# A graph layer's messages: two silus in one ScalarE operation, edge addresses made once, and more columns copied per step

## The chip, the cores and the metric

The kernel runs on one core of a Trainium2 chip. The metric is the device time of one execution in microseconds (us), the median of the runs shown. The engines are TensorE (PE for its products, PEld for its weight loads), VectorE (DVE), ScalarE (ACT), GpSimd (POOL) and SyncE (SP, which only issues DMAs here). An engine's own queue, in which its register loads and its DMA issues stand, is written with a q: DVEq, ACTq, SPq.

## The reference

One layer of a message-passing network over 12500 nodes of 64 features and 400000 edges that are sorted by their target `dst`, with 16 features on each edge:

```
m_in = concatenate([x[src], x[dst], edge_attr], axis=-1)
h = silu(m_in @ W1 + b1)
messages = silu(h @ W2 + b2)
agg = segment_sum(messages, dst, num_segments=12500)
x = layernorm(x + silu(concatenate([x, agg]) @ W3 + b3))
```

W1 is 144 x 64. Its first 64 rows belong to x[src], the next 64 (called W1b here) to x[dst], the last 16 to the edge features.

## The kernel before

**Tiling.** The edges lie in 3125 tiles of 128. Eight tiles are an octet, and there are 391 octets; three octets are a chunk. One loop (line 644) runs over the octets, and inside it the order of the work on PE, ACT, DVE and SP is the order in which the code is written: each of these engines does its share of turn o in that order, and waits in that order. POOL runs by itself, up to three octets ahead. Because the edges are sorted, an octet's targets lie in a window of 48 consecutive nodes.

**First layer of an octet** (line 475). `xw` holds, for the window of the octet, x W1b of its 48 nodes (twice, for even and odd tiles) and W1's rows for the edge features; its product with `oh` (a 0/1 comparison of `dst` with the window's nodes, and the edge features under it) gives the target and edge parts of all 1024 edges in one PSUM bank, `p1` (line 482). The source part is added tile pair by tile pair. For most tiles POOL has fetched the rows of x W1a by indirect DMA from a table `pa` in DRAM, 128 rows an instruction (line 391), and PE adds them through the identity (line 495). The first 12 octets (RAW) fetch x itself, while the tables are still being made.

**Columns.** For about half of the octets the first tile pair isn't fetched by POOL. Its 256 columns of x transposed are copied out of `xs`, a copy of x in SBUF, into `cx`, one 64 x 4 byte copy per edge, by DVE (`tensor_reduce`, line 316) and by ACT (`copy`, line 318), and PE multiplies them by W1a (line 492). Each turn DVE copies 40 columns and then 32 (VCOLS), ACT 32 and 32 (ACOLS). The address of a column comes from a register: the registers are loaded up to eight at a time from a row of addresses (LOADS, line 299), and the eight copies follow. The row is fetched three turns ahead from `src_row` by SP (`index`, line 369) and is turned from node numbers to byte addresses by two small DVE operations (`address`, line 377). `xs` holds x twice, in partitions 0 to 63 and 64 to 127, and edges of the pair's second tile are copied from the upper half to the upper half of `cx`; so the two halves of an address row need different bases (XBASE). A few further tile pairs are fetched row by row by SP (line 342).

**Silus and second layer.** ACT applies silu with bias `b1s` to `p1` (line 499), giving `h`. One turn later PE forms b2 + h W2 in `p2` (lines 508 and 510), and ACT applies silu again (line 514), giving the messages `m`. One turn later again PE adds them up by node with the comparison `eh` (line 523, `add_up`), and two turns after that DVE adds the window's sums into `agg` (line 528, `add_window`).

**Order within turn o.** PE: the window product of o+1 (only for o+1 < 60), first layer of o, `add_up` of o-2, second layer of o-1. ACT: 32 columns, silu of o, 32 columns, silu of o-1. DVE: `add_window` of o-4, comparison `oh` of o+1 (line 465), 40 columns, comparison `eh` of o+1 (line 471), 32 columns, `address` of o+2 if an address row begins there. From octet 60 on, x W1b of a window is loaded by SP from a DRAM table `pw1b`, which is made in turns 8 to 57 (`table_b`); before that PE makes it from x (`window_product`) and DVE copies it (line 443).

**Node part.** As soon as a group of 512 nodes has all of its edges, PE forms its products with W3 (lines 555 to 558), ACT the silu (line 564), DVE the statistics and the division (lines 571 to 588), between the turns of the edges.

Of the kernel before, what the change touches and what calls it, by code (L numbers as in the profile page):

```python
# [20 lines left out]
P = 128  # L21
G = 4
CT = 24
OT = 8
# [7 lines left out]
TABLES = 7  # L32
ACOLS = (32, 32)
VCOLS = (40, 32)
ROWS = 16
LOADS = 8
XBASE = (0, 64 << 18)
XADDR = 36864
LAG = CT * P // 32
# [6 lines left out]
@with_exitstack  # L46
def kernel(
    ctx: ExitStack,
    tc: tile.TileContext,
    x: bass.AP,  # L50
    xt: bass.AP,
    src_c: bass.AP,
    src_row: bass.AP,
    dst_c: bass.AP,
    dst_row: bass.AP,
    attr_t: bass.AP,
    dst_2: bass.AP,
    attr_2: bass.AP,
    base: bass.AP,
    w1: bass.AP,  # L60
    b1: bass.AP,
    w2: bass.AP,
    b2: bass.AP,
    w3: bass.AP,
    b3: bass.AP,
    out: bass.AP,
    edges: int,
):

    nc = tc.nc
    N, D = x.shape

    const = ctx.enter_context(tc.tile_pool(name="const", bufs=1))
    dram = ctx.enter_context(tc.tile_pool(name="dram", bufs=1, space=DRAM))
    pa = dram.tile([N, D], F32, name="pa")

    pw1b = dram.tile([xt.shape[1], 2 * D], F32, name="pw1b")
    badi = const.tile([1, 1], I32, name="badi")
    ident = const.tile([P, P], F32, name="ident")  # L90
    make_identity(nc, ident)

    with ExitStack() as inner:
        windows(inner, tc, ident, badi, pa, pw1b, x, xt, src_c, src_row, dst_c, dst_row, attr_t, dst_2, attr_2, base, w1, b1, w2, b2, w3, b3, out, edges)

    flag = nc.values_load(badi[0:1, 0:1], min_val=0, max_val=2 * P,
                          skip_runtime_bounds_check_because="a count of partitions")
    with tc.If(flag > 0):
        general(tc, ident, x, xt, src_c, dst_c, dst_row, attr_t, w1, b1, w2, b2, w3, b3, out, edges)


def windows(ctx, tc, ident, badi, pa, pw1b, x, xt, src_c, src_row, dst_c, dst_row, attr_t, dst_2, attr_2, base, w1, b1, w2, b2, w3, b3, out, edges):
    nc = tc.nc
# [31 lines left out]
    nc.vector.memset(w1d, 0.0)  # L135
    b1s = const.tile([P, 1], F32, name="b1s")
    w2d = const.tile([P, P], F32, name="w2d")
    nc.vector.memset(w2d, 0.0)
    w3s = const.tile([P, D], F32, name="w3s")
    for s in range(2):  # L140
        h = slice(s * D, (s + 1) * D)
        nc.scalar.dma_start(w1d[h, h], w1[0:D, :])
        nc.scalar.dma_start(b1s[h, :], b1.rearrange("(k o) -> k o", o=1))
    XC = 2048
    xs = fast.tile([P, NP], F32, name="xs")

    def resident(s, c):
        w = min(XC, NP - c)
        nc.scalar.dma_start(xs[s * D:(s + 1) * D, c:c + w], xt[:, c:c + w])

    resident(0, 0)
    for s in range(2):
        h = slice(s * D, (s + 1) * D)
        nc.scalar.dma_start(w2d[h, h], w2)
    resident(0, XC)
    w3x = const.tile([D, D], F32, name="w3x")
# [38 lines left out]

    agg = fast.tile([P, NP], F32, name="agg")

    bf = fast.tile([1, NO], F32, name="bf")
# [58 lines left out]
    with tc.tile_pool(name="gat", bufs=AHEAD + 2) as gat, tc.tile_pool(name="drp", bufs=2) as drp, \  # L257
# [3 lines left out]
            tc.tile_pool(name="ps1", bufs=2, space=PSUM) as ps1, \  # L261
            tc.tile_pool(name="ps2", bufs=2, space=PSUM) as ps2, \
            tc.tile_pool(name="psa", bufs=1, space=PSUM) as psa, \
# [33 lines left out]
        def addresses(eng, j, e0, n):  # L297
            s = e0 // P
            _, regs = nc.values_load_multi_w_load_instructions(  # L299
                indices[j][0:1, e0:e0 + n], engines=(eng,), min_val=XBASE[s] + XADDR,  # L300
                max_val=XBASE[s] + XADDR + 4 * (N - 1), skip_runtime_bounds_check_because="src names a node")
            return regs

        def columns(o, eng, part):
            for j, e0, n in pieces(o, eng, part):
                regs = addresses(eng, j, e0, n)
                if pairs[j] not in cols:
                    cols[pairs[j]] = cx.tile([P, P], F32, name="cx")
                t = cols[pairs[j]].bitcast(U8)
                s = e0 // P  # L310
                h = slice(s * D, (s + 1) * D)
                for e, r in zip(range(e0 % P, e0 % P + n), regs):
                    to, frm = t[h, 4 * e:4 * e + 4], xb[h, ds(r - (XBASE[s] + XADDR), 4)]
                    if eng == ENG.DVE:

                        nc.vector.tensor_reduce(to, frm[:, :, None], AX.X, OP.max)  # L316
                    else:
                        nc.scalar.copy(to, frm)  # L318
# [46 lines left out]
        def index(o):  # L365
            for j in begun(o):
                t = cxi.tile([1, 2 * P], I32, name="cxi")
                e = octs[pairs[j]][1] * P
                nc.sync.dma_start(t, src_row[:, e:e + 2 * P])
                indices[j] = t  # L370

        def address(o):
            for j in begun(o):
                t = indices[j]
                for s in range(2):
                    h = slice(s * P, (s + 1) * P)
                    nc.vector.tensor_scalar(t[:, h], t[:, h], 4.0, float(XBASE[s] + XADDR), op0=OP.mult, op1=OP.add)  # L377

# [26 lines left out]
        def table_b(c):  # L405
# [5 lines left out]
            for i in range(k):  # L411
                p = min(P, n - i * P)
                nc.tensor.matmul(ps[:p, i, :], xs[0:D, c + i * P:c + i * P + p], w1ab[:, 1, :], start=True, stop=True)
            if n == 2 * P:
# [21 lines left out]
        def window_product(o):  # L436
            pw = mis.tile([P, P], F32, name="mm")
            nc.tensor.matmul(pw[:E, :], winrow[o].rearrange("k s w -> k (s w)"), w1bb.rearrange("k s m -> k (s m)"),
                             start=True, stop=True)
            winrow[o] = pw  # L440
# [14 lines left out]

        hots = {}

# [17 lines left out]
        def first_layer(o):  # L475
# [4 lines left out]
            oh, eh = hots.pop(o)  # L480
            p1 = ps1.tile([P, OT // 2, P], F32, name="p1")
            nc.tensor.matmul(p1[:, :k], xw[o % XWB], oh, start=True, stop=False, skip_group_check=True)  # L482
            if o < RAW:
                pt = mis.tile([P, OT // 2, P], F32, name="mm")
                for i in range(k):
                    nc.tensor.matmul(pt[:, i, :], ga[:, 2 * i:2 * i + 2, :].rearrange("p s d -> p (s d)"), ident,
                                     start=True, stop=True)
                xg = work.tile([P, OT // 2, P], F32, name="m")
                nc.vector.tensor_copy(xg[:, :k], pt[:, :k])
# [3 lines left out]
            for i in range(1 if o in pairs else 0, k if o >= RAW else 0):  # L493
                g2 = single.pop(o) if o in rpairs and i == 1 else ga[:, 2 * i:2 * i + 2, :]
                nc.tensor.matmul(p1[:, i, :], g2.rearrange("p s d -> p (s d)"), ident,  # L495
                                 start=False, stop=(i == k - 1), skip_group_check=True)
            columns(o, ENG.Activation, 0)
            h = work.tile([P, OT // 2, P], F32, name="h")
            nc.scalar.activation(h[:, :k], p1[:, :k], AF.Silu, bias=b1s)  # L499
            made[o] = h, eh  # L500

        def second_layer(o):
            c, t0, n, first, last = octs[o]
            n2 = n + n % 2
            k = n2 // 2
            h, eh = made.pop(o)
            p2 = ps2.tile([P, OT, D], F32, name="p2")
            nc.tensor.matmul(p2[:, :n2, :], one3, b2r[:, :n2, :], start=True, stop=False, skip_group_check=True)  # L508
            for i in range(k):
                nc.tensor.matmul(p2[:, 2 * i:2 * i + 2, :].rearrange("p s d -> p (s d)"), h[:, i, :], w2d,  # L510
                                 start=False, stop=(i == k - 1), skip_group_check=True)
            columns(o + 1, ENG.Activation, 1)
            m = work.tile([P, OT, D], F32, name="m")
            nc.scalar.activation(m[:, :n2], p2[:, :n2], AF.Silu)  # L514
            made[o] = m, eh

        def add_up(o):
            c, t0, n, first, last = octs[o]
            m, eh = made.pop(o)
            pg = sums[:, o % 4, :]  # L520
# [120 lines left out]
        with tc.manual_schedule(engines={ENG.PE, ENG.Activation, ENG.DVE, ENG.SP}):  # L641
            compare_dst(0)
            compare_nodes(0)
            for o in range(NO + 1):
                if o == 0:
                    sources(0, slice(CT, SCT))
                    nc.sync.dma_start(dc[:, CT:SCT], dst_c[:, CT:SCT])
                for k in parts[3 * o - 3:3 * o] if o else []:
                    n = min(XC, NP - k)
                    nc.scalar.activation(agg[:, k:k + n], zero.to_broadcast([P, n]), AF.Copy)  # L650
                if o < 2:
                    for c in parts[2:5] if o == 0 else parts[5:]:
                        resident(0, c)
                if o == 3:
# [6 lines left out]
                if o == RAW:  # L661
                    nc.vector.memset(mv, 1.0)
                    nc.vector.memset(eps, 1e-5)
                if 5 <= o < 5 + (len(parts) + 1) // 2:
                    for c in parts[(o - 5) * 2:(o - 4) * 2]:
                        resident(1, c)
                index(o + 3)
# [18 lines left out]
                if o < NO:  # L686
                    first_layer(o)
                if o == 0:
                    nc.vector.tensor_copy(b2r, b2p[:, None, :].to_broadcast([3, OT, D]))
# [14 lines left out]
                if o >= 1:  # L704
                    for c in tables[(o - 1) * per:o * per]:
                        table(c)
                if 8 <= o < 8 + len(tables_b):
                    table_b(tables_b[o - 8])
                if o >= 2:
                    add_up(o - 2)  # L710
                if o >= 1:
                    second_layer(o - 1)
                address(o + 2)
                raddress(o + 2)
# [296 lines left out]
```

## Time and profile before

| | |
|---|---|
| time, median of 3 runs | 3724.96 us (3719.63 to 3726.66) |
| time of the execution that was profiled | 3726.66 us |
| its span, first to last instruction | 3724.9 us |
| busy in the span: PE, PEld, DVE, ACT, POOL | 69%, 51%, 73%, 78%, 68% |
| granted TensorE clock | 0.712 |
| DMA: bytes moved, mean rate | 243.80 MB, 65 GB/s |

A row of the costliest groups reads: line, engine, operation, the tiles it writes and reads, how often; then its busy time and the mean duration of one; then the idle time of the engine just before such instructions and what ended most of it. Instructions of one kind overlap on DVE and ACT, so that the busy time of a group can be less than count times mean. "issue" means that the engine waited for nothing that the profile shows. The loop takes 9 to 10 us a turn after the first 150 us.

### The profile page before, as it was taken

To read this page: it belongs to the slowest core of one execution; us is meant where nothing else is said; L and a number is where in the kernel's file an instruction comes from. 1 tells how busy PE (TensorE), PEld (TensorE's weight loads), DVE (VectorE), ACT (ScalarE), POOL (GpSimd) and SP (SyncE) were. 2 spreads that over 40 slices of the span, in tenths; PEclk is the share of its full clock that TensorE was granted. 3 is DMA by queue.
4 is the path that set the end of the run, shared out by engine and by line. 5 is a ranking of instruction groups with operands and counts; after the bars stand their busy time and mean duration, and the time that the engine had idled before them with its cause. 6 is when DMAs were issued, how large, how long until landed. Compare 5 with 4: busy or idle time off the path is not lost. (4 is left out here: it accounts for less than half of the span.)

```text
span 3724.9 us, 112677 instructions
## 1 busy us (share of the span) xinstructions
PE 2581.7 (69%) x14667; PEld 1910.2 (51%) x14667; DVE 2703.3 (73%) x29014; ACT 2912.8 (78%) x24892; POOL 2535.2 (68%) x2690
## 2 busy tenths in 40 slices
PE   7878777767766667666666666667767666667666
PEld 5655555545544545454554555545545455445454
DVE  2477777777777777777777777777777777777775
ACT  2477878788787878878888878887888887887885
POOL 7777666676666766767666676676676666766763
PEclk8766667676667667777777777777766777776767
DMA  6533332322322232222232232232222222223222
GB/s 131 115 71 76 68 67 63 67 59 57 69 60 61 60 66 58 60 64 61 59 64 66 59 68 56 60 65 59 60 62 63 66 57 62 63 58 67 58 59 53
DMA packets 201259, 243.80 MB, mean 65 GB/s; under 512 B 87009, under 2 KB 139806, under 8 KB 199598
## 3 DMA queue, kind: packets, MB, share of 16 engines
q1 hardware_dynamic: 86336, 130.74, 15.0%
q0 software_dynamic: 85792, 88.02, 12.8%
q10 hardware_dynamic: 28366, 17.75, 1.9%
q14 instruction: 640, 5.24, 0.5%
q8 instruction: 125, 2.05, 0.2%
HBM read 223.41 MB, written 12.87 MB: 63 GB/s over the span
## 5 line engine op out<-in xcount | busy, mean ns | idle before, releaser
L391 POOL DMA_INDIRECT ga<-pa,sc x2585 | 2442.3, 945 | 1111.0 <-issue 683.9
L316 DVE TENSOR_REDUCE cx<-xs 64x4 uint8 x26944 | 2058.4, 148 | 813.8 <-issue 764.3
L318 ACT COPY cx<-xs 64x4 uint8 x24000 | 2403.6, 188 | 133.8 <-issue 102.2
L523 PE MATMUL pg<-eh,m 128*64 128x48 f32 x6250 | 357.2, 273 | 1047.3 <-DVE agg L528 996.7
L523 PEld LDWEIGHTS pg<-eh,m 128*64 128x64 f32 x6250 | 309.0, 184 | 1108.1 <-issue 630.5
L510 PE MATMUL p<-w2d,h 128*128 128x128 f32 x3126 | 743.6, 413 | 0.0
L510 PEld LDWEIGHTS p<-w2d,h 128*128 128x128 f32 x3126 | 633.9, 301 | 143.5 <-issue 143.5
L482 PE MATMUL p<-oh,xw 128*128 128x512 f32 (+1 forms) x782 | 672.8, 959 | 27.8 <-DVE xw L443 27.6
L514 ACT ACTIVATE m<-p 128x512 f32<-128x512 f32 x391 | 232.9, 596 | 443.1 <-PE p L510 427.4
L495 PEld LDWEIGHTS p<-ident,ga 128*128 128x128 f32 x2586 | 448.5, 248 | 160.5 <-issue 147.2
L495 PE MATMUL p<-ident,ga 128*128 128x128 f32 x2586 | 439.4, 321 | 0.0
L499 ACT ACTIVATE h<-p,b1s 128x512 f32<-128x512 f32 x391 | 267.1, 683 | 54.9 <-PE p L490 41.5
L465 DVE TENSOR_TENSOR oh<-dr,wrow 96x512 f32<-96x512 int32 x391 | 263.2, 673 | 2.8 <-DMA dr<-in_dst 2.8
L482 PEld LDWEIGHTS p<-oh,xw 128*128 128x128 f32 x782 | 197.9, 310 | 43.0 <-DVE xw L443 34.7
L471 DVE TENSOR_TENSOR eh<-wrow,dc 128x384 f32<-128x384 f32 x391 | 213.9, 547 | 2.4
L508 PE MATMUL p<-b2r,one 3*128 3x512 bf16 x391 | 207.1, 530 | 0.0
L492 PEld LDWEIGHTS p<-cx,w1d 128*128 128x128 f32 x398 | 115.6, 290 | 177.8 <-issue 177.8
L528 DVE TENSOR_TENSOR agg<-agg,pg 128x48 f32 x391 | 78.0, 200 | 102.6 <-PE pg L523 46.3
L391 POOL DMA_INDIRECT ga<-in_x,sc x96 | 90.8, 945 | 30.3 <-issue 27.4
L564 ACT ACTIVATE z<-mm 128x256 f32<-128x256 f32 (+1 forms) x25 | 9.6, 383 | 125.5 <-PE mm L558 125.5
L492 PE MATMUL p<-cx,w1d 128*128 128x128 f32 x398 | 104.6, 357 | 0.0
L377 DVE TENSOR_SCALAR cxi<-cxi 1x128 int32<-1x128 int32 x398 | 75.9, 242 | 0.8
(86 smaller groups left out, 766.1 us busy)
## 6 DMA issues: line engine op xcount, KB each, us to landing
rx<-pa SPq DMA_DIRECT2D x5888, 0.2 KB
dr<-in_dst SPq DMA_DIRECT2D x260, 288.0 KB
ga<-pa,sc POOLq DMA_INDIRECT x2585
oh<-in_attr SPq DMA_DIRECT2D x130, 192.0 KB
xw<-pw1b SPq DMA_DIRECT2D x331, 48.0 KB
pw1b<-pbs ACTq DMA_DIRECT2D x49, 128.0 KB
xs<-in_xt ACTq DMA_DIRECT2D x12, 512.0 KB
cxi<-in_src_row SPq DMA_DIRECT2D x199, 1.0 KB
```

The costliest lines, as they stand in the source:

```text
L316: nc.vector.tensor_reduce(to, frm[:, :, None], AX.X, OP.max)
L318: nc.scalar.copy(to, frm)
L391: nc.gpsimd.indirect_dma_start(out=ga[:, i, :], out_offset=None, in_=x if o < RAW else pa[:, :], in_offset=bass.IndirectOffsetOnAxis(ap=sc ...
L465: nc.vector.tensor_tensor(oh[:E, :], dr[:, e:e + w], wn[:E, o:o + 1].to_broadcast([E, w]), op=OP.is_equal)
L471: nc.vector.tensor_tensor(eh[:, :n], row[:, None, :].to_broadcast([P, n, S]), rel[:, t0:t0 + n, None].to_broadcast([P, n, S]), op=OP.is_equal)
L482: nc.tensor.matmul(p1[:, :k], xw[o % XWB], oh, start=True, stop=False, skip_group_check=True)
L492: nc.tensor.matmul(p1[:, 0, :], w1d, cols.pop(o), start=False, stop=False, skip_group_check=True)
L495: nc.tensor.matmul(p1[:, i, :], g2.rearrange("p s d -> p (s d)"), ident, start=False, stop=(i == k - 1), skip_group_check=True)
L499: nc.scalar.activation(h[:, :k], p1[:, :k], AF.Silu, bias=b1s)
L510: nc.tensor.matmul(p2[:, 2 * i:2 * i + 2, :].rearrange("p s d -> p (s d)"), h[:, i, :], w2d, start=False, stop=(i == k - 1), skip_group_ch ...
L514: nc.scalar.activation(m[:, :n2], p2[:, :n2], AF.Silu)
L523: nc.tensor.matmul(pg[s * D:(s + 1) * D, :], m[:, i, :], eh[:, i, :], start=(i < 2), stop=(i >= n - 2), skip_group_check=True)
```

## The change

The change has four parts that belong together.

1. **b1 moves into the tables.** A product of a row of ones with `b1r` is added to x W1b when `pw1b` and the windows are made, so that `p1` already holds b1. The silu of the first layer needs no bias any more.
2. **Both silus in one operation.** `p1` of octet o and `p2` of octet o-1 lie next to each other in one PSUM tile `p12` of two banks, and one activation of 128 x 1024 (`silus`) makes `h` of o and `m` of o-1. PE now does the second layer of o-1 right after the first layer of o, and `add_up` of o-2 after it. ACT does all of its columns of a turn before the one activation.
3. **Addresses made once.** At the start `src_row` is loaded across 128 partitions into the still unused `agg`, multiplied and shifted in one DVE operation of 128 x 3125, and stored to `adr` in DRAM (`addresses_made`, in turn 1). `index` fetches rows of `adr`; `address` is gone. `agg` is zeroed in another order, so that the part in use comes last.
4. **x once in SBUF, and more columns.** `xs` keeps only partitions 0 to 63; columns for the upper half of `cx` are read from the lower half of `xs`. ACT copies 40 + 32 = 72 columns a turn, DVE 40 + 36 = 76.

```diff
-ACOLS = (32, 32)
-VCOLS = (40, 32)
+ACOLS = (40, 32)
+VCOLS = (40, 36)
...
+    adr = dram.tile([1, TILES * P], I32, name="adr")
+    at = agg[:, :TILES].bitcast(I32)
+
+    def addresses_made():
+        nc.vector.tensor_scalar(at, at, 4.0, float(XADDR), op0=OP.mult, op1=OP.add)
+        nc.sync.dma_start(adr.rearrange("o (p j) -> (o p) j", p=P), at)
...
-                    to, frm = t[h, 4 * e:4 * e + 4], xb[h, ds(r - (XBASE[s] + XADDR), 4)]
+                    to, frm = t[h, 4 * e:4 * e + 4], xb[:D, ds(r - XADDR, 4)]
...
-                nc.sync.dma_start(t, src_row[:, e:e + 2 * P])
+                nc.sync.dma_start(t, adr[:, e:e + 2 * P])
...
-        def address(o):
-            for j in begun(o):
-                t = indices[j]
-                for s in range(2):
-                    h = slice(s * P, (s + 1) * P)
-                    nc.vector.tensor_scalar(t[:, h], t[:, h], 4.0, float(XBASE[s] + XADDR), op0=OP.mult, op1=OP.add)
...
             nc.tensor.matmul(pw[:E, :], winrow[o].rearrange("k s w -> k (s w)"), w1bb.rearrange("k s m -> k (s m)"),
-                             start=True, stop=True)
+                             start=True, stop=False)
+            nc.tensor.matmul(pw[:E, :], ones[:, :E], b1r.rearrange("o s k -> o (s k)"), start=False, stop=True)
...
+            both[o] = ps1.tile([P, 2, OT // 2, P], F32, name="p12")
+            outs[o] = work.tile([P, 2, OT // 2, P], F32, name="hm")
...
-            columns(o, ENG.Activation, 0)
-            h = work.tile([P, OT // 2, P], F32, name="h")
-            nc.scalar.activation(h[:, :k], p1[:, :k], AF.Silu, bias=b1s)
...
-            columns(o + 1, ENG.Activation, 1)
-            m = work.tile([P, OT, D], F32, name="m")
-            nc.scalar.activation(m[:, :n2], p2[:, :n2], AF.Silu)
...
+        def silus(o):
...
+            columns(o, ENG.Activation, 0)
+            columns(o, ENG.Activation, 1)
...
+                nc.scalar.activation(hm, pp, AF.Silu)
...
+                if o >= 1:
+                    second_layer(o - 1)
+                silus(o)
                 if 8 <= o < 8 + len(tables_b):
                     table_b(tables_b[o - 8])
                 if o >= 2:
                     add_up(o - 2)
-                if o >= 1:
-                    second_layer(o - 1)
-                address(o + 2)
```

## The prediction

> **What bounds the kernel now.** I read the waits first, because 69 to 78 per cent busy on four engines says nothing about which one the others follow. VectorE's waits, longest first (who waited, for what: us in total, times, longest):
>
> ```profile
> DVE cx L316 <- issue: 764.3, 2399, 0.7
> DVE m L489 <- PE mm L486: 71.1, 12, 11.9
> DVE agg L528 <- PE pg L523: 46.3, 14, 7.3
> DVE agg L528 <- PE mm L558: 33.7, 21, 8.0
> ```
>
> Nothing holds DVE in the loop: 764.3 us of its idle time lie in front of its own column copies and end with nothing but issue. Waits for other engines sum to some 160 us, of which L489 and most of L523 lie in the first 150 us. The others do wait, and along a line that begins at DVE:
>
> ```profile
> PE pg L523 <- DVE agg L528: 996.7, 307, 7.6
> ACT m L514 <- PE p L510: 427.4, 274, 4.0
> POOL ga L391 <- PE p L495: 370.2, 163, 12.3
> ```
>
> PE's `add_up` waits for DVE's `add_window`, the first thing DVE does in a turn; ACT's silu waits for the second layer behind it; POOL waits for PE to give back gather buffers. So DVE leads. One turn of it, from the timeline of DVE (start, duration, in brackets the idle time before it):
>
> ```profile
> 2020.14 0.68 DVE L465 TENSOR_TENSOR oh<-dr,wrow 96x512 f32<-96x512 int32 x1
> 2020.85 1.33 DVE L316 TENSOR_REDUCE cx<-xs 64x4 uint8 x16
> 2022.48 0.62 DVE L316 TENSOR_REDUCE cx<-xs 64x4 uint8 x8 [0.30 <-issue]
> ...
> 2027.19 0.59 DVE L316 TENSOR_REDUCE cx<-xs 64x4 uint8 x8 [0.32 <-issue]
> 2028.12 0.59 DVE L316 TENSOR_REDUCE cx<-xs 64x4 uint8 x8 [0.34 <-issue]
> 2028.64 0.41 DVE L377 TENSOR_SCALAR cxi<-cxi 1x128 int32<-1x128 int32 x2
> 2029.13 0.20 DVE L528 TENSOR_TENSOR agg<-agg,pg 128x48 f32 x1
> ```
>
> The turn has no slack: work, or a gap of 0.30 us ahead of a group of eight copies. The gap is the load of the next eight registers, as the source view of line 299 shows (duration min/median/max in ns):
>
> ```profile
> L299 DVEq TENSOR_LOAD <-cxi x3368: 591/596/866, 147.9 to 3682.7; - x199
> ```
>
> A load of eight registers takes 596 ns. Groups follow each other every 0.92 us (2027.19 to 2028.12), so the queue needs 0.92 - 0.596 = 0.33 us to hand out eight copies, 0.041 us each, and only then loads again; the copies last 0.6 us and cover the rest of the load: 0.33 + 0.596 - 0.6 = 0.32 us of gap. Behind a long operation (`oh`) a second group follows without one. Of 3368 groups 2399 show a gap, 764.3 / 2399 = 0.319 us each. The chain of waits agrees: before its last 40 us, which are PE's, it runs through DVE's copies and these gaps.
>
> **The change, part by part.** I sum for DVE and check that no other engine gets above it.
>
> *More columns on DVE.* Running the kernel's own rule for pieces with both settings: a turn gets 136 columns before and 148 after, so pairs go from 199 to 217, DVE's copies from 26944 (as in the page) to 28500, and its register groups from 3368 to 3809. Of the 441 new groups some 375 are a turn's last four columns (36 is four groups of eight and one of four), the rest pieces that now cut a tile's border. The page's row:
>
> ```profile
> L316 DVE TENSOR_REDUCE cx<-xs 64x4 uint8 x26944 | 2058.4, 148 | 813.8 <-issue 764.3
> ```
>
> 2058.4 / 26944 = 76.4 ns a copy; 1556 more are +119 us. Each new group adds a load, and none of the operations that cover loads is added. But a load of four is shorter. The source view of line 399, which loads four window bases every fourth turn, shows it:
>
> ```profile
> L399 DVEq TENSOR_LOAD <-bi x98: 339/344/756, 33.6 to 3692.2; - x98
> ```
>
> 344 ns for four and 596 for eight are 63 a register and 92 besides. Behind a group of eight, a load of four leaves a gap of 0.33 + 0.344 - 0.6 = 0.07 us: 375 x 0.07 = +26 us. A cut group (4 + 4 for 8) has gaps of 0.07, then 0.16 + 0.344 - 0.3 = 0.20, then 0.16 + 0.596 - 0.3 = 0.45 ahead of the next eight, 0.72 in place of twice 0.32: some 60 x 0.1 = +6 us. Together +32 us. Bounds: all gaps covered, 0; or the queue as the limit throughout, with loads 1556 x 0.063 + 441 x 0.092 = 139 and handing out 1556 x 0.041 = 64, so +203 in place of 119 + 32 = 151.
>
> The Trainium skill ("DMA: Bandwidth & Descriptors", Latency and other measured facts) gives a tensor load a floor of about 600 ns, which would speak against groups of four: each new group would show the full 0.319 us, 441 x 0.319 = +141 us in place of 32, and the forecast would be 109 us later. The 344 ns above are under that floor, and I go by them.
>
> *`address` goes.* 398 operations, 75.9 us busy. From DVE's timeline, turns between octets 120 and 380 without node work have a median of 9.31 us where `address` runs and 9.08 us where it doesn't: 0.23 us in 199 turns, -46 us, which I take; -77 at most. It hardly waits (0.8 us idle before it in all), so no stall goes with it.
>
> *Reading x from the lower half.* No copy in this trace crosses from one half of the partitions to the other, so this is a bound: a copy lasts 148 ns but a new one starts every 76; if a crossing copy didn't overlap with the one before, 14250 x 72 ns = +1020 us. The nearest rows, the same copies within a half, say 0 and I take 0. The Trainium skill ("VectorE: DVE Perf Modes", Two Vector instructions with no wait between them) holds an instruction only where its input or its output starts in another quadrant than the one last read or last written, each compared with its own predecessor: by that a run of crossing copies is held once, at its first, as runs in the upper half are today. The sum by it is the one I use.
>
> *Start.* One DVE operation on 128 x 3125: by the small address rows (242 ns for 128 elements, 283 for 256) 1.2 us, by the subtraction on `dc` (533 ns for 368) 4.5 us; I take 3. It waits for a 1.6 MB load, and ACT's zeroing of part of `agg` in turn 2 for a 1.6 MB store. Between 0 and 50 us the DMA moved 158 GB/s, so each costs about 10 us of that stream, while DVE has 11.9 us of idle time in turn 2 (L489) to hide the first. SP stands in its issue of the store till DVE has finished, with the loads of later windows behind it. Against that, 3.2 MB of the second copy of x (turns 5 to 8) go. I take +10, from 0 to +30. The products with `b1r` are on PE: 60 for windows and 100 for the table, at 0.3 to 0.4 us (L413, L438), hidden from turn 12 on and in the +10 before.
>
> *PE's order.* `add_up` and a node group's product (8 x 0.65 us) no longer stand behind the second layer, 2.7 us with its bias product (L508, L510), so `agg` is free sooner than DVE's next `add_window`: of the 33.7 us I take -25, from 0 to -34.
>
> *ACT.* +3052 copies x 0.100 us (2403.6 / 24000) = +305 us. The silus cost 683 and 596 ns; at 0.82 ns an element (596 for 512, 491 for 384) one of 1024 is 1016 ns, -0.26 us x 390 = -103. Busy 2913 + 202 = 3115 us, 8.0 us a turn and some 0.4 us of exposed loads and table work, under DVE's 9.5. Its one wait is for PE, which after `add_window` needs add_up 1.1, first layer 2.8, second layer 2.7, while ACT copies for 7.2 us. Behind that wait stand the next turn's 72 copies, whose pair PE takes up a turn or two after its last copy, and a node group's silu, which now waits for the product without other work between. So ACT gains nothing that shows, and loses nothing.
>
> *POOL* makes 36 gathers fewer (18 pairs of two tiles) at 1.25 us, 45 us that lie in its waits for PE. The rows fetched by SP stay.
>
> Sum: 119 + 32 - 46 + 10 - 25 = +90 us on the profiled execution's 3726.7 (span 3724.9 and 1.8 around it), 3817; the median of runs is 1.7 us under that execution: **3815 us**, slower by 2.4%. By the bounds: 119 + 0 - 77 + 0 - 34 = +8 (3733) to 203 - 46 + 30 - 0 = +187 (3912).
>
> **The rivals.**
>
> *DVE's queue limits throughout* (0.24). For it: turns of 9.08 us are close to 9 x 0.92 plus the handing out of six other instructions. Against: a division of 0.98 us makes a turn some 0.7 us longer, more than its handing out could, and two groups behind `oh` run without a gap. +203 - 46 + 10 - 25 = +142: 3867.
>
> *The new loads are hidden wholly* (0.10), because DVE's queue gets ahead where `address` goes. 119 - 46 + 10 - 25 = +58: 3783. Against it: the part ahead of `eh` shows the same 3.8 gaps a turn with `address` in front of it and without.
>
> *POOL is the pace* (0.09): 2681 gathers at 0.945 us busy and 0.30 us issue are 3338 us, nearest to the span after DVE when its issue counts; DVE's gaps would then be elastic. 36 gathers fewer give -45 us, 3680, faster. It decides from the point where PE's L495 waits for gathers; the trace has 13.0 us of that in all, and POOL itself waits 370 us for PE.
>
> *Crossing copies don't overlap* (0.02): 3815 + 1020, some 4830. The change then doesn't do what it says: one copy of x doesn't serve as two did.
>
> **How the numbers follow.** The forecast has 0.55. Faster by over 0.2% (about what a measurement of this kernel can tell from no change) only by POOL's case: 0.09. Within 0.2%: where the forecast's costs all lie at their low ends (+8 us), 0.03 of its 0.55. Slower: 0.88. The range 3740 to 3890 holds the forecast's case but for its two ends, nearly all of the queue's case and the hidden loads, and leaves out the other two.
>
> **What would show it.** Right: DVE's L316 near 28500 copies and 2180 us busy, with issue idle near 800 before it; a group of four at the end of a turn, with a gap under 0.1 us ahead of it; ACT's silu 1.0 us; PE still waiting for `agg` L528 and DVE for nobody. Wrong: issue idle that stays at 764 or passes 850, DVE waiting for ACT or PE in the loop, copies that no longer overlap, or a first column much later than 148 us.

## The result and the profile after

The changed kernel takes 3906.23 us (median of 4 runs, 3900.97 to 3916.37); the kernel before took 3722.3 us beside it (4 runs, 3715.76 to 3726.66). The ratio is 1.0499, 95% interval 1.047 to 1.0528: slower by 184 us, where +90 was forecast. The profiled execution took 3909.7 us with a span of 3907.7. In the first three sets of experiments the kernel before itself took 5.4 to 5.5 ms instead of 3.72, for a reason that stayed open; of those only the ratios to the kernel before on the same chip are used, and times below are from the others unless said.

VectorE's waits in the changed kernel (who waited, for what: us in total, times, longest) answer to those shown of before:

```profile
DVE cx L322 <- issue: 834.9, 2521, 0.7
DVE agg L543 <- PE pg L538: 76.9, 20, 12.1
DVE hm L492 <- PE mm L489: 64.0, 12, 16.6
...
DVE agg L543 <- PE mm L573: 6.1, 3, 2.8
```

The picture is the same: from turn 58 on DVE waits for hardly anything but its own issue (70 of the 76.9 us that it waits for `add_up`, PE's line 538, lie before that turn). The idle time before its copies has grown from 764.3 to 834.9 us, and the wait for a node group's product has fallen from 33.7 to 6.1. The other engines' lines:

```profile
PE pg L538 <- DVE agg L543: 1009.3, 304, 5.7
ACT hm L524 <- PE p L513: 326.5, 185, 9.2
POOL ga L390 <- PE p L498: 597.2, 222, 13.5
```

PE still waits for DVE's `add_window`, ACT behind PE, and POOL, with 36 gathers fewer to make, waits 227 us longer for its buffers. So DVE still leads over most of the span. One of its turns, from DVE's timeline:

```profile
2013.34 0.68 DVE L466 TENSOR_TENSOR oh<-dr,wrow 96x512 f32<-96x512 int32 x1
2014.05 0.60 DVE L322 TENSOR_REDUCE cx<-xs 64x4 uint8 x8
2014.88 0.60 DVE L322 TENSOR_REDUCE cx<-xs 64x4 uint8 x8 [0.23 <-issue]
...
2018.24 0.56 DVE L472 TENSOR_TENSOR eh<-wrow,dc 128x384 f32<-128x384 f32 x1
2018.82 1.29 DVE L322 TENSOR_REDUCE cx<-xs 64x4 uint8 x16
2020.44 0.60 DVE L322 TENSOR_REDUCE cx<-xs 64x4 uint8 x8 [0.33 <-issue]
2021.36 1.01 DVE L322 TENSOR_REDUCE cx<-xs 64x4 uint8 x12 [0.32 <-issue]
2022.40 0.20 DVE L543 TENSOR_TENSOR agg<-agg,pg 128x48 f32 x1
```

Three things are to be seen. The turn ends with twelve copies without a visible gap: eight and then the new four, together 1.01 us where eight take 0.60, so the four cost 0.41 us. `address` no longer stands ahead of `add_window`. And the second group behind `oh`, which ran without a gap in the turn shown of before, has one of 0.23 us here. The page's row of the copies:

```profile
L322 DVE TENSOR_REDUCE cx<-xs 64x4 uint8 x28500 | 2153.1, 141 | 904.5 <-issue 834.9
```

2153.1 / 28500 is 75.5 ns a copy: half of these copies cross from the lower to the upper half, and they overlap as the others do.

Where the time went is read best by stages. I cut each span at DVE's comparison `oh`, once in every turn (from DVE's timeline; us of each stage, and in brackets the mean turn):

| kernel (columns of ACT, DVE) | before turn 13 | turns 13-58 | turns 58-120 | turns 120-380 | rest |
|---|---|---|---|---|---|
| before (64, 72) | 147.9 | 444.8 (9.89) | 582.3 (9.39) | 2439.8 (9.38) | 110.0 |
| after (72, 76) | 171.0 | 493.7 (10.97) | 602.8 (9.72) | 2524.4 (9.71) | 115.8 |
| cols_before_3 (64, 72) | 163.6 | 454.0 (10.09) | 568.9 (9.18) | 2374.1 (9.13) | 105.9 |
| dve64_act72_2 (72, 64) | 182.3 | 502.7 (11.17) | 563.4 (9.09) | 2351.7 (9.05) | 100.4 |
| act80_dve64 (80, 64) | 171.3 | 521.5 (11.59) | 572.6 (9.24) | 2357.4 (9.07) | 110.7 |
| no_b1_2 (72, 76) | 148.8 | 494.1 (10.98) | 602.7 (9.72) | 2524.2 (9.71) | 116.1 |
| two_silus (72, 76) | 164.2 | 494.9 (11.00) | 602.3 (9.72) | 2524.2 (9.71) | 115.3 |
| cxi4_2 (72, 76) | 172.7 | 505.9 (11.24) | 602.8 (9.72) | 2522.4 (9.70) | 114.9 |

Of the 183 us between the spans of before and after, 23 lie before turn 13, 49 in turns 13 to 58, in which the table of x W1b is made, and 111 behind them.

### The profile page after: what moved, and what is told of

Its sections match the earlier page's. It is cut to its first block, busy times and chain, and to the rows that moved or that the text cites. A ratio compares the mean times of both kernels' runs of the same rounds, so it can differ in the third digit from the quotient of the medians.

```text
span 3907.7 us, 116590 instructions
## 1 busy us (share of the span) xinstructions
PE 2706.5 (69%) x14985; PEld 1930.4 (49%) x14985; DVE 2749.6 (70%) x30173; ACT 3120.1 (80%) x27555; POOL 2500.0 (64%) x2654
## 4 chain that ended last, share of the span: by engine, by line
DVE 44%; issue 20%; SPq 9%; PE 9%; DVEq 7%; ACT 6%; DMA 5%; ACTq 1%
DVE cx L322 35%; DVEq L305 7%; ACT cx L324 5%; SPq L348 5%; DVE eh L472 3%; SPq L344 2%; DVE oh L466 2%; DMA rx<-pa 2%; PE p L485 1%; PE p L513 1%; PE pg L538 1%; ACTq L305 1%; DVE agg L543 1%; PE mm L185 1%; SPq L429 1%
## 5 line engine op out<-in xcount | busy, mean ns | idle before, releaser
L324 ACT COPY cx<-xs 64x4 uint8 x27052 | 2694.5, 189 | 141.0 <-issue 116.1
L322 DVE TENSOR_REDUCE cx<-xs 64x4 uint8 x28500 | 2153.1, 141 | 904.5 <-issue 834.9
L538 PE MATMUL pg<-eh,hm 128*64 128x48 f32 x6250 | 378.7, 286 | 1016.0 <-DVE agg L543 1009.3
L538 PEld LDWEIGHTS pg<-eh,hm 128*64 128x64 f32 x6250 | 319.5, 196 | 1084.6 <-DVE agg L543 1068.4
L485 PE MATMUL p<-oh,xw 128*128 128x512 f32 (+1 forms) x782 | 757.0, 1069 | 3.9 <-DVE xw L444 2.9
L524 ACT ACTIVATE hm<-p 128x1024 f32<-128x1024 f32 x389 | 397.4, 1022 | 329.8 <-PE p L513 326.5
L498 PEld LDWEIGHTS p<-ident,ga 128*128 128x128 f32 x2550 | 550.6, 303 | 153.3 <-issue 147.6
L513 PE MATMUL p<-w2d,hm 128*128 128x128 f32 x3126 | 513.6, 313 | 99.5 <-ACT hm L524 99.4
L498 PE MATMUL p<-ident,ga 128*128 128x128 f32 x2550 | 554.4, 384 | 0.0
L513 PEld LDWEIGHTS p<-w2d,hm 128*128 128x128 f32 x3126 | 436.0, 216 | 230.5 <-ACT hm L524 121.2
L543 DVE TENSOR_TENSOR agg<-agg,pg 128x48 f32 x391 | 79.3, 203 | 127.8 <-PE pg L538 76.9
```

The lines of the kernel that those rows point to most:

```text
L524: nc.scalar.activation(hm, pp, AF.Silu)
L538: nc.tensor.matmul(pg[s * D:(s + 1) * D, :], m[:, i, :], eh[:, i, :], start=(i < 2), stop=(i >= n - 2), skip_group_check=True)
```

## The experiments

Three explanations stood against each other: that the added columns on DVE cost more than forecast; that something else of the change costs (b1's products, the one activation, the rows of addresses); and that another engine leads in a stage. Expectations in microseconds of the 3.72 ms scale are to be compared with the first sets of runs by their difference to the kernel before, in per cent. Even so the sizes don't carry over: in the 5.5 ms runs the added columns make some 3 per cent (after_again against cols_before, below), in the others 6.2 (1.0499 against 0.9877). So the first sets show which part costs, and not how much.

### The columns

**cols_before, cols_before_2, cols_before_3**: the changed kernel with the numbers of columns of before.

```diff
-ACOLS = (40, 32)
-VCOLS = (40, 36)
+ACOLS = (32, 32)
+VCOLS = (40, 32)
```

> The changed kernel with the columns of before: 64 a turn on ACT, 72 on DVE. Theory A (DVE's columns set the loop from turn 60 on, ACT's set the turns 8 to 57): a loop turn loses the 0.41 us of its group of four and the cover it took, and the address operations stay away, so turns 120 to 380 fall from 9.71 to about 9.2 us on average, turns 13 to 60 fall from 10.9 to about 10.1, and only the start (22 us later than before in the changed kernel) remains: 3680 us, between 3660 and 3710. Theory B (the rest of the change costs, by the order of PE's work, the one silu or the start, whatever the columns): 3760 us or more, with loop turns above 9.4.

> The changed kernel with the columns of before (ACT 64, DVE 72), once more. Where the kernel before takes about 3722 us. Theory A (columns): loop turns (120 to 380) of about 9.2 us, turns 13 to 60 of about 10.1, the start 22 us late: 3680 us, between 3660 and 3710. Theory B (order, one silu, start): 3760 us or more. Where the kernel before takes 5.5 ms, engines are held up by something that the two theories don't hold, and the run says again only that both have the same time.

> The changed kernel with the columns of before (ACT 64, DVE 72), in the conditions of the result. Theory A: loop turns (120 to 380) of 9.2 us, turns 13 to 57 of about 10.1, the start 22 us late: 3680 us, between 3660 and 3710, ratio 0.983 to 0.997. Theory B (order, one silu, start): 3760 us or more.

Measured: 0.9986 of before (0.997 to 1.0003) and 0.9966 (0.9945 to 0.9987) in the 5.5 ms runs; beside a kernel before of 3.72 ms it takes **3672.18 us** (3662.04 to 3688.14; before 3724.96), ratio 0.9877 (0.9834 to 0.9921). So all of the loss comes with the columns, and the rest of the change gains 53 us. After less cols_before_3 is 234 us in the medians, 241 in the spans: by stages +7, +40, +34, +150 and +10. The row of the copies on the page of cols_before_3:

```profile
L322 DVE TENSOR_REDUCE cx<-xs 64x4 uint8 x26944 | 2017.9, 141 | 841.9 <-issue 794.2
```

Against the row of after this is 135 us less busy for 1556 copies fewer (forecast 119) and 63 us less idle time ahead of them (forecast 32).

**dve76_act64, dve72_act72**: only DVE's four columns, or only ACT's eight.

```diff
-ACOLS = (40, 32)
+ACOLS = (32, 32)
```
```diff
-VCOLS = (40, 36)
+VCOLS = (40, 32)
```

> The changed kernel with 64 columns a turn on ACT and 76 on DVE. Theory A: the loop keeps DVE's turn of 9.7 us; turns 13 to 60 lose 8 copies of 0.1 us on ACT, 47 x 0.8 = 38 us: 3870 us, between 3850 and 3885. A theory in which DVE sets every turn (A1): the same time as the changed kernel, 3906. A theory in which ACT's columns set the loop (A2): under 3700.

> The changed kernel with 72 columns a turn on ACT and 72 on DVE. Theory A: loop turns as with the columns of before, 9.2 us, turns 13 to 60 near 10.7 us because ACT still copies 72: 3715 us, between 3690 and 3740. A1: the same as the changed kernel with the columns of before. A2: near 3900.

Measured, on one chip in the 5.5 ms runs: 1.0205 (1.0179 to 1.023) with DVE's four, 0.9894 (0.9869 to 0.9919) with ACT's eight, 0.9986 with neither. There DVE's four columns cost 2.2 per cent, and ACT's eight beside 72 on DVE gain 0.9. The second goes against the expectation, by which ACT's eight were to cost some 35 us; in the 3.72 ms runs they weren't tried alone beside 72.

**before_dve76, before_dve76_2**: the kernel before with DVE's four columns.

```diff
-VCOLS = (40, 32)
+VCOLS = (40, 36)
```

> The kernel before with 76 columns a turn on DVE instead of 72 and nothing else changed. Theory A: each turn from 60 on is 0.4 to 0.5 us longer, the early ones less, since ACT sets part of them: 3880 us, between 3850 and 3900. If DVE's queue covers the new loads by itself (the rival of the prediction with hidden loads): 3722 + 119 x 0.6, under 3800. If POOL were the pace: under 3722.

> The kernel before with 76 columns a turn on DVE, once more. Theory A: 0.4 to 0.5 us a turn from turn 60 on, less before: 3880 us where the kernel before takes 3722, ratio 1.034 to 1.05. New loads hidden: ratio under 1.02. POOL the pace: under 1.

Measured, in the 5.5 ms runs: 1.0264 (1.0233 to 1.0295) and 1.0216 (1.0174 to 1.0257). On this scale the four columns cost the old kernel about what they cost the new one; they need no partner in the change. The expected 1.034 to 1.05 was not reached.

**dve64_act72, dve64_act72_2, act80_dve64**: ACT keeps its 72 columns or gets 80, DVE has 64.

```diff
-VCOLS = (40, 36)
+VCOLS = (32, 32)
```
```diff
-ACOLS = (40, 32)
-VCOLS = (40, 36)
+ACOLS = (40, 40)
+VCOLS = (32, 32)
```

> The changed kernel with 72 columns a turn on ACT and 64 on DVE, so the same 136 as before, shifted to ACT. Theory A: DVE's turn loses a whole group of eight (0.92 us) and its group of four, and falls to about 8.4 us; ACT's turn is 72 copies of 0.1 us, a silu of 1.0 and its wait for PE, about 8.6; POOL's is 6.8 gathers of 1.25, 8.5. So the loop falls to about 8.7 to 8.9 us a turn, turns 13 to 60 stay near 10.7 with ACT: 3722 - 330 x 0.5 + 22 + 40 = 3600 us, between 3540 and 3680. Theory B: no lower than the run with the columns of before.

> The changed kernel with 72 columns a turn on ACT and 64 on DVE, in the conditions of the result. Theory A: DVE's turn falls to 8.4 us, ACT's stays at 72 x 0.098 + 1.02 + 0.3, 8.4, and POOL's is 6.8 gathers of 1.25, 8.5: loop turns of 8.7 to 9.0 us, turns 13 to 57 near 10.7: 3600 us, between 3540 and 3680. If the order of PE or the one activation holds the loop up, no lower than with the columns of before.

> The changed kernel with 80 columns a turn on ACT and 64 on DVE. Theory A: ACT becomes the bound at 80 x 0.098 + 1.02 + 0.3, 9.2 us a turn, with turns 13 to 57 at 11 us and more: where the kernel before takes 3722 us about 3700, and slower than the run with 72 and 64. If ACT had room for 80 columns beside DVE's 8.4 us: faster than that run, ratio under 0.975.

Measured: dve64_act72 0.9821 (0.978 to 0.9861) in the 5.5 ms runs; dve64_act72_2 3690.1 us beside 3724.96, 0.9889 (0.9847 to 0.993); act80_dve64 3728.63 beside 3723.98, 1.0011 (0.999 to 1.0033). The expectation that the turns would go on shrinking with DVE's columns fell: eight columns fewer than cols_before_3 bring the loop only from 9.13 to 9.05 us, and the time is no better. DVE's waits in dve64_act72_2 show what took its place:

```profile
DVE cx L322 <- issue: 682.9, 2089, 0.7
DVE oh L466 <- DMA dr<-in_dst: 207.7, 87, 4.9
DVE agg L543 <- PE pg L538: 139.2, 38, 10.0
```

The issue idle falls by 111 us as it should, but `oh` now waits 208 us for the DMA that brings `dst`, a wait of 5.9 us in cols_before_3. SP issues that load between its row fetches; two rows of SP's timeline in dve64_act72_2:

```profile
2000.54 0.79 SPq L454 DMA_DIRECT2D dr<-in_dst  x2
...
2004.38 6.59 SPq L348 DMA_DIRECT2D rx<-pa  x16
```

Sixteen row fetches hold SP for 6.59 us of a turn of 9. That this is what makes `dst` late is argued from the order alone; it wasn't tried. With 80 columns ACT comes to the front, as PE's wait in act80_dve64 shows:

```profile
PE p L513 <- ACT hm L524: 675.6, 288, 7.9
```

The chains of waits on the pages of after, dve64_act72_2 and act80_dve64, by engine in shares of the span, say the same:

```profile
DVE 44%; issue 20%; SPq 9%; PE 9%; DVEq 7%; ACT 6%; DMA 5%; ACTq 1%
```

```profile
SPq 23%; ACT 19%; PE 19%; DMA 13%; DVE 11%; issue 10%; ACTq 3%; DVEq 1%; POOL 1%; POOLq 0%
```

```profile
ACT 37%; SPq 19%; PE 15%; DMA 10%; issue 7%; DVE 6%; ACTq 5%; DVEq 1%; POOL 1%; POOLq 0%
```

DVE carries most of after's chain; in dve64_act72_2 no single engine does.

These two runs decide what leads in after: with the same 72 columns ACT can turn in 9.05 us, so the 9.71 us of after from turn 58 on are not ACT's. Before turn 58 it is the other way round: the mean turn is 10.09 us with 64 columns on ACT, 10.97 and 11.17 with 72, 11.59 with 80, whether DVE copies 76 or 64.

### ACT in turns 13 to 58

The stage needed no kernel of its own. By the groups of ACT in it, in after and then in cols_before_3 (count, busy us, mean ns, idle before):

```profile
L324 ACT COPY cx<-xs 64x4 uint8 x3240 | 330.0, 188 | 106.1 <-issue 97.5 <-DVE cx L322 2.4 <-DMA rx<-pa 1.4
L524 ACT ACTIVATE hm<-p 128x1024 f32<-128x1024 f32 x45 | 45.8, 1018 | 0.6
```

```profile
L324 ACT COPY cx<-xs 64x4 uint8 x2894 | 294.3, 189 | 85.9 <-issue 67.8 <-DMA rx<-pa 10.5 <-DVE xw L444 2.8
```

In after the silu waits 0.6 us for PE in 45 turns: here ACT does not follow PE. That the stage lengthens with ACT's columns, whatever DVE copies, says that ACT leads in it, though not alone, as its stores show below. It has 346 copies more than in cols_before_3, 35.7 us; the stage is 40 us longer. ACT's timeline in after shows what else fills these turns:

```profile
583.05 1.02 ACT L524 ACTIVATE hm<-p 128x1024 f32<-128x1024 f32 x1
583.97 0.26 ACT L415 COPY pbs<-mm 128x128 f32<-128x128 f32 x1
586.51 0.38 ACTq L416 DMA_DIRECT2D pw1b<-pbs  x1
587.54 7.28 ACT L324 COPY cx<-xs 64x4 uint8 x72 [3.31 <-issue]
594.73 1.01 ACT L524 ACTIVATE hm<-p 128x1024 f32<-128x1024 f32 x1
```

Each turn ACT copies a piece of the table (L415) and issues its store (L416), and only about 1.0 us after that issue come the next copies. The issue stands 0.03 to 5.9 us behind the end of L415. What holds it back can be read from the trace's semaphore records. In 21 of the 44 recorded turns it is over 0.25 us late, 57 us in all, and each time ACT's queue stands just before it at a wait that ends 37 or 38 ns after a DMA of SP's has landed on the same semaphore: 20 times a row fetch (L348), once a load of edge features (L455). This store and SP's DMAs count their landings on the same eight semaphores. So ACT does wait for another engine's transfers here. The same delays make 29 us of the stage in before, 35 in cols_before_3, 66 in cxi4_2 and 69 in dve64_act72_2; these last two have the stage 12 and 9 us longer than after.

### The first layer's bias in the tables

**no_b1, no_b1_2**: the changed kernel without the products with `b1r`, so that b1 is left out of the result.

```diff
-                nc.tensor.matmul(..., w1ab[:, 1, :], start=True, stop=False)
-                nc.tensor.matmul(ps[:p, i, :], ones[:, :p], b1r[:, 0, :], start=False, stop=True)
+                nc.tensor.matmul(..., w1ab[:, 1, :], start=True, stop=True)
...
-                             start=True, stop=False)
-            nc.tensor.matmul(pw[:E, :], ones[:, :E], b1r.rearrange("o s k -> o (s k)"), start=False, stop=True)
+                             start=True, stop=True)
```

> The changed kernel without the two products that add b1 to the tables; b1 is left out of the result. If these products on PE make the start and turns 13 to 60 late: the start comes back by some 10 to 20 us and the early turns by up to 30, 3860 to 3880 us. If ACT's 72 copies and its one silu set the early turns (theory A): only the start's share, 3885 to 3900 us.

> The changed kernel without the two products that add b1 to the tables (b1 is left out of the result), in the conditions of the result. If these products make the start and the early turns late: 3860 to 3885 us, with turn 13 some 10 to 20 us earlier. If ACT fills the early turns and the start waits for other things: within 10 us of 3906.

Measured: 1.0208 (1.0162 to 1.0254) in the 5.5 ms runs; then 3880.59 us beside 3724.96, 1.0428 (1.0396 to 1.0461), 26 us under after. The stages put nearly all of it before turn 13: 148.8 us instead of 171.0, and next to nothing later. The first stage by engine, in after, no_b1_2 and before (from and to, length, then busy us and instructions of PE, PEld, DVE, ACT and POOL, the granted clock, DMA share, GB/s):

```profile
0.00:171.00 171.00, 138.77 (x687) 99.33 (x687) 35.79 (x100) 32.77 (x37) 121.33 (x134) 0.75 0.52 121
```

```profile
0.00:148.80 148.80, 115.38 (x645) 83.07 (x645) 35.85 (x100) 32.32 (x37) 111.78 (x124) 0.83 0.59 136
```

```profile
0.00:147.90 147.90, 114.97 (x635) 82.54 (x635) 34.23 (x102) 34.06 (x47) 109.92 (x123) 0.83 0.63 137
```

PE is the busiest engine of this stage. With the products it has 42 matmuls and 23 us more, and the stage is 22 us longer; of after's chain of waits in it 136 of 171 us are PE's. The mean granted clock is lower too, 0.75 instead of 0.83, but that doesn't decide it: with the same products the stage takes 171.3 us in act80_dve64 at 0.87 and 164.2 in two_silus at 0.86. The other runs with these products begin turn 13 at 163.6 to 182.3 us, so some 15 to 33 us is what can be said. no_b1_2 also has the 1.6 MB load and store of the addresses and begins turn 13 only 1 us after before. That is net of the second copy of x that goes, and of the rest of the change; its chain of waits runs through the load of the addresses for 13.5 us, so the transfers are not shown to be free.

### The rows of addresses, the one activation

**after_again, cxi4, cxi4_2, cxi4_64_72**: the changed kernel again; with a fourth buffer for the address rows, for which `rowi` gives up its own place; and that with DVE's 64 columns.

```diff
-    rowi = fast.tile([P, S], I32, name="rowi")
+    rowi = agg[:, :S].bitcast(I32)
...
-            ... tc.tile_pool(name="cxi", bufs=3) as cxi, \
+            ... tc.tile_pool(name="cxi", bufs=4) as cxi, \
```

> The changed kernel itself, beside the kernel before in the same conditions as the experiments. If theory A (the added columns of DVE) holds, it stands to the run without b1's products and to the one with 64 columns on ACT and 76 on DVE as those do to each other: within 30 us of both, and some 130 to 150 us above the run with the columns of before. If the one silu, the order of PE or the start were most of it, the run with the columns of before would have kept most of the loss, so this run would be under 60 us above it.

> The changed kernel with four buffers for address rows instead of three. Theory C (early turns): with 148 columns a turn a row is used up every 1.73 turns, so that SP, which fetches three turns ahead, stands in front of a row buffer that ACT or DVE hasn't finished (99 us between 171 and 685 us of the profiled run after, 41 us in the same turns before), and what SP issues later comes late, among it what ACT's table store waits for. Then these waits of SP nearly vanish and turns 13 to 57 fall from 10.97 us by 0.3 to 0.8 us, 15 to 35 us in all. Theory A alone (ACT's own work fills the early turns): the same time within 10 us.

> The changed kernel with four buffers for address rows, in the conditions of the result. Theory C: SP no longer stands before a full row buffer in turns 13 to 57 (99 us of its waits between 171 and 685 us of the profiled run after); these turns fall from 10.97 by 0.3 to 0.8 us: 15 to 35 us less than 3906. If ACT's own work alone fills them: the same time within 10 us.

> As the kernel with four row buffers, with 72 columns a turn on ACT and 64 on DVE. Theory A: nine fewer DVE columns in two fewer groups give the loop turns of 8.7 to 8.9 us where the kernel before has 9.38; where the kernel before takes 3722 us: 3560 us, between 3500 and 3640, ratio 0.94 to 0.98. If ACT takes over as the bound at 72 columns: turns of 9.2 and more, ratio above 0.985.

Measured, in the 5.5 ms runs: after_again 1.0282 (1.0233 to 1.0332), cxi4 1.0277 (1.0223 to 1.0331), cxi4_64_72 0.9875 (0.9819 to 0.9932), above its 0.94 to 0.98 (DVE has twelve columns fewer there, not nine). Then cxi4_2 3922.69 us beside 3724.96, 1.0546 (1.051 to 1.0582). The theory that late rows of addresses, or SP's wait for a free buffer, lengthen turns 13 to 58 finds no support: with a fourth buffer SP's wait for one falls from 101 to 69 us in these turns, and the stage is 505.9 us instead of 493.7.

**address_loop**: the changed kernel, but the rows of addresses come from `src_row` and are turned into addresses in the loop.

```diff
-                nc.sync.dma_start(t, adr[:, e:e + 2 * P])
+                nc.sync.dma_start(t, src_row[:, e:e + 2 * P])
...
+                    nc.vector.tensor_scalar(t[:, h], t[:, h], 4.0, float(XADDR), op0=OP.mult, op1=OP.add)
...
-                    addresses_made()
+                address(o + 2)
```

> The changed kernel, but with the addresses made per row by two DVE operations in the loop, as before, and no address table at the start. Prediction's step: the loop gets 217 x 0.23 = 50 us longer, the start up to 10 us shorter: +40 us against the changed kernel. If DVE's queue covers these operations or their removal only exposes loads: within 15 us of it.

Measured, in the 5.5 ms runs: 1.0395 (1.0342 to 1.0448), 59 us over after_again on the same chip. Addresses made once are worth about 59 us there; the forecast had 46, and the expectation for this run 40, with the start in it.

**two_silus**: the changed kernel with the silu always as two activations of 128 x 512.

```diff
-            if k == [OT // 2, OT // 2]:
+            if False:
```

> The changed kernel with its one activation of 128 x 1024 split into two of 128 x 512 over the same tiles, at the same place. Theory A: ACT gets 0.17 us a turn longer (596 x 2 - 1020 ns), nothing that shows in the loop turns, in which ACT still waits for PE; turns 13 to 57, which ACT fills, get up to 45 x 0.17 = 8 us longer: +0 to +10 us against the changed kernel. If the one activation itself (two PSUM banks held for both halves at once, PE waiting for both) made part of the loss, this run is faster than the changed kernel by over 20 us.

Measured: 3902.71 us (3902.59 to 3911.29) beside 3723.98, 1.0497 (1.046 to 1.0533), against 1.0499 of after. The silus' rows, of after from the page and of two_silus from the groups:

```profile
L524 ACT ACTIVATE hm<-p 128x1024 f32<-128x1024 f32 x389 | 397.4, 1022 | 329.8 <-PE p L513 326.5
```

```profile
L528 ACT ACTIVATE hm<-p 128x512 f32<-128x512 f32 x782 | 422.5, 591 | 310.4 <-PE p L513 297.5 <-PE p L493 9.6
```

Fusing them saves 25 us of ACT's busy time and no time of the kernel that can be measured: the time saved turns into waiting for PE.

## Why the prediction was right or wrong

**What led was right, but not in every stage.** DVE sets the pace from turn 58 on; in turns 13 to 58 ACT does, with SP's fetches ahead of its stores, and the prediction did not look at that stage by itself. The chain of waits that it called in agreement could not show it: in the profile of before that chain begins at 3615 us and covers the last 110 us of the span.

**"More columns on DVE" is the term that was mis-sized**: +151 us for 376 turns, 0.40 us a turn. From turn 120 to 380 it was 0.58 (9.71 against 9.13). The groups of DVE in these 260 turns show the copies, in after and then in cols_before_3:

```profile
L322 DVE TENSOR_REDUCE cx<-xs 64x4 uint8 x19760 | 1493.5, 141 | 630.7 <-issue 583.5 <-ACT hm L524 1.7 <-DMA rx<-pa 0.6
```

```profile
L322 DVE TENSOR_REDUCE cx<-xs 64x4 uint8 x18720 | 1402.0, 141 | 585.7 <-issue 553.8 <-ACT cx L324 2.4 <-ACT hm L524 1.0
```

Busy: +91.5 us for 1040 copies, 88 ns each, where 76.4 had been taken, the mean of copies in groups of eight. Inside a group a copy starts every 64 ns and takes 140 (medians in after), so four take about 3 x 64 + 140 = 332 ns, 83 each: the tail of a group weighs more on a short one. The 0.41 us of the last four in the timeline, with any small gap inside, are of that size. Idle: +45 us, 0.17 a turn, where 0.085 had been taken. The gap ahead of the four was sized rightly: it makes only 5 us in these 260 turns, and the shortest load takes 339 ns. But the gaps grew elsewhere too: by 11 us ahead of the second group behind `oh`, by 12 ahead of the groups behind `eh`, those at cut borders among them, and by 16 in gaps under 0.15 us, too short to be listed. From turn 58 to the end the columns cost 194 us; 0.40 a turn would have been 133. The queue's bound, +203 or 0.54 a turn, lies nearer to the measurement than the value taken. That the queue limits throughout isn't shown by this: taking `address` out would then have saved little more than its handing out, and address_loop and the 0.25 us a turn below speak against that.

**"ACT gains nothing that shows, and loses nothing" failed in turns 13 to 58.** The prediction's 8.0 us a turn is a mean over the span. In this stage ACT is busy 8.48 us a turn in after and has 2.5 us of gaps, most of them issue behind the table's stores, which 1.3 us a turn stand waiting for SP's DMAs. The trace of before would have told it. The same stage there, by engine:

```profile
147.90:592.70 444.80, 355.88 (x1922) 258.50 (x1921) 334.10 (x3527) 351.72 (x3019) 307.55 (x325) 0.68 0.32 70
```

ACT is busy for 351.7 of 444.8 us, more than DVE's 334.1, and 79.4 us of its idle time there are issue, nearly all of it behind the table's stores: 9.6 of 9.9 us a turn were taken. The added columns cost 40 us there; ACT's 346 copies more are 35 of them at the 0.100 us a copy that the prediction itself had. The 1% that this adds to the time was thought to be hidden.

**The start** cost 23 us against +10 (0 to 30): inside its bounds, but for another reason. The transfers of the addresses, to which the prediction gave the weight, leave 1 us net in no_b1_2. The products with `b1r`, which it put "in the +10", are on the path, because PE's work is most of the chain of waits there.

**The gains were right.** Without the columns the change gives -53 us (-58 in the spans) where -46 + 10 - 25 = -61 was forecast. Behind turn 58 it is -83 us, 0.25 a turn, where 46 + 25 over 376 turns make 0.19. The wait for a node group's product fell by 28 us in after, where 25 had been taken; `address` by itself is known only from the 5.5 ms runs. How the two share in the 83 us isn't settled. In turns 13 to 58 the same version is 9 us slower than before though ACT's silus are cheaper. ACT's wait for a node group's product is 18.1 us there, against 1.9 in before, and its stores are late by 35 us against 29; whether that makes the 9 us stays open.

**Copies that cross the halves** overlap. Told apart by the kernel's order of columns, the 14252 crossing copies of after take 141.7 ns in the mean, the others 139.9; in before those within the upper half took 155.5. The Trainium skill ("VectorE: DVE Perf Modes", Two Vector instructions with no wait between them) led to the same sum. Its floor of about 600 ns for a tensor load ("DMA: Bandwidth & Descriptors", Latency and other measured facts) does not hold here: the loads of four registers lie under it, at 339 ns for the shortest.

**The range** missed by 16 us at its top. The rival of the queue (3867), plus the 40 us of ACT's stage, would have been 3907, near the 3906 measured: the first of the two costs stood in a rival alone, the second in no case. The agreement is partly luck, since the start and the gains behind turn 58 were off as well.

**The best version** is the change without its columns: cols_before_3, 3672.18 us, 0.9877 of before (0.9834 to 0.9921).

## What to carry to other kernels

Cut the loop into its stages before saying which engine has room: an average of 8.0 us a turn hid a stage in which ACT had 0.3 us left. When work is added to the engine that leads, price it at its own granularity, with the tail of a short group and with the cover that its neighbours lose, and not by the mean of full groups: 0.58 us a turn came out instead of 0.40. When a change has parts of both signs, run it without the part that loads the leading engine; here the other parts, which gain 53 us together, stood behind one that costs 234.

## What the runs showed of the hardware that was not expected

One engine's DMA issue can stand behind another's transfers: ACT's store of the table waited 57 us in turns 13 to 58 of after for landings of SP's DMAs that are counted on the same semaphores. The view of the waits lists this time as "issue" ahead of ACT's copies.

A register load's time goes by the number of registers: the loads of DVE take 596 ns for eight and 339 at the shortest, for four; ACT's 546 and 305. The source view of the loads in after (duration min/median/max in ns):

```profile
L305 DVEq TENSOR_LOAD <-cxi x3809: 339/596/899, 170.9 to 3869.1; - x191
L305 ACTq TENSOR_LOAD <-cxi x3486: 305/546/1031, 170.9 to 3862.4; - x194
```

In the runs in which the kernel before took 5.4 to 5.5 ms, operations and loads kept their durations (cols_before_2: loads of DVE 591/596/877 ns), but DVE's issue idle was 1908.9 us instead of 794.2 and ACT's 1574.6 instead of 83.6. Now and then both engines handed out only one copy every 0.72 us, in the same moments, and one set of sixteen row fetches held SP for 11.87 us in cols_before_2 (6.59 in dve64_act72_2 above). POOL showed no such steps: its issue idle was 685.5 us, against 725.0. What does that was not found.
